# Output and down products with the tokens stationary in a linear-attention kernel gated by a Hadamard feed-forward net

## The chip, the cores and the metric

The kernel runs on one core of one Trainium2 chip. All numbers are 32-bit floats. The metric is device time in microseconds, the median of some runs; beside it stands one execution under the hardware profiler, whose span is the time from the first to the last instruction.

The engines are TensorE (PE, matrix products into PSUM; its weight loads are counted apart as PEld), VectorE (DVE), ScalarE (ACT), GpSimd (POOL) and SyncE (SP), which issues nearly all of this kernel's transfers.

## The reference

`x` has the shape (8, 512, 512): 8 batches of 512 tokens of 512 features. After a layer norm there are two branches, and the result is a gated residual. `fwht` is the normalized Walsh-Hadamard transform over the features.

```python
xn = layernorm(x)
# branch s: linear attention
q, k, v = xn @ Wq.T + bq, xn @ Wk.T + bk, xn @ Wv.T + bv
kv = cumsum((elu(k) + 1) * v, axis=tokens)              # elementwise
s = ((elu(q) + 1) * kv * 32 ** -0.5) @ Wo.T + bo
# branch g: feed-forward net, 512 -> 2 x 2048 -> 512
h = fwht(xn * SU_ug)
h = silu((h @ W_gate.T) * Wscale_gate) * ((h @ W_up.T) * Wscale_up)
h = fwht(h * SU_dp)
g = silu((h @ W_down.T) * Wscale_dp)
out = x + s * g
```

## The kernel before

**Tiling.** The batches are worked off in four pairs `p`; the two batches of a pair are the two sides `s` of a 2x2 block product. Each product is done as a Strassen-Winograd scheme: seven products P1 to P7 of blocks stand for eight, and sums before and after are done on other engines. The contraction is cut in units of 2 x 128 features, of which attention and the output projection have two and down has eight (four in each half).

**A group.** `group` (L265) makes one pair of 128-wide output tiles for all tokens: for each of the seven products a 128x128 block of the weight is loaded as the stationary side and 512 tokens move past it (the matmul is L277). Results have features on the partitions and tokens in the columns. The PSUM tile `px` (three banks) gathers P1, P6, P5 and P3 one after another, and its state is read in between as `sa`, `sb`, `sc` (on ScalarE at L289 or, with a bias added, at L291; on VectorE at L287 where an earlier half is added). `py` (one bank) takes P2, `pz` (two banks) takes P7 and P4; VectorE adds them to the snapshots (L295). A further pair of PSUM banks is tagged `t`, for transposes and for the folding of weights.

**Order.** An agenda (`at`, `advance`) places the seven products of a group in time, so that products of neighbouring groups lie between each other and snapshots are ready when they are needed; its unit is the product of one 128x128 block with 512 tokens. Within that, a scheduler that knows dependencies and priorities fixes the order on each engine; `background()` marks work of a lower priority. Each engine then follows its own list in order and waits at each instruction for what it needs.

**Weights.** `get_w` takes the next weight from a list in the order of use and asks for three ahead (`ask`). In the first pair weights come raw from the input, are encoded for the seven products (`encode_weights`, L175 to L179), and the encoded form is stored to HBM; later pairs read it back (`later_w`). For gate and up the Hadamard transform is folded into the weights: butterflies on VectorE, one product with the 128x128 Hadamard matrix `had` on TensorE (`pw`), a copy with scale on ScalarE. For down the same is done on four blocks `o` of 128 output columns: `butterflies_down` (its load of `rd` from HBM L691, its butterflies L646 and L647) and `fold_down` (the product `pwd` L702, the copies L708, the store to `wd_f` L711). `between`, called after each group, counts groups: at 0, 3, 6 and 9 it puts butterflies, at 2, 5, 8 and 11 a fold. In later pairs gate and up use a two-level scheme with 256 moving columns (`block_product`, product L364), and their weights are streamed.

**Output projection and down.** `project_out` makes two groups `g` with the bias from ScalarE, and stores `o` to HBM. In the first pair it stands after the first gate group. `down` makes two groups in each of two halves of the hidden features. The first half's sum is stored to HBM; it is fetched again with `s` and `x` (as `y`) before the second half. The first group of each half has an `early` part, contraction units that can be multiplied before the last hidden unit `ho` is there (3 of 4 in the first pair, else 2). In the second half each quarter of `d` gets the Silu with the scale `wsc_c` (ScalarE, L604) and is multiplied with `s` (L607, on POOL for g = 0 and VectorE for g = 1). `finish` (L632) then turns the product to rows of tokens with 32 transposes `po` (L638), adds `y` on VectorE (L639) and stores 8 times 256 KB.

**Transfers.** All loads and stores but a few constants are issued on SP's queue, in one order; an issue that waits for data holds up those behind it. The pool `t8` has six buffers of 1 MB each, `wpool` four for weights; x of the next pair has one buffer.

## Time and profile before

| | |
|---|---|
| median of 3 runs | 1608.95 us (1608.57 to 1610.97) |
| profiled execution | 1611.34 us, span 1609.6 us |
| mean granted clock of TensorE | 0.992 |
| TensorE busy | 1559.2 us in 4944 instructions |
| VectorE busy | 920.8 us in 1314 |
| ScalarE / POOL busy | 452.4 / 475.6 us |
| moved by DMA | 246.30 MB, q1 45.3% of 16 engines |
| stores of out | 32 of 256 KB |

A group's row gives the line, the engine and the operation, the output and the inputs by the program's names, the shape and the count, then busy time, the mean of one in ns, the engine's idle time just before and what ended it. A row of the chain gives start, duration and what ran or landed. A matmul of 32-bit floats stands in the trace as two instructions. The mean duration of a matmul includes its latency; what counts is the distance between starts.

### The profile page before, as it was taken

Reading aid. Unit: us, or ns where it says so; the run is one execution under the profiler, and the core shown is the slowest. Engines: PE = TensorE matmul, PEld = TensorE weight load, DVE = VectorE, ACT = ScalarE, POOL = GpSimd, SP = SyncE. Lnnn points to the kernel's source line nnn. Section 1 sums busy time; section 2 is a strip of 40 time slices with the busy share of each in tenths; the row PEclk is TensorE's granted clock in tenths of the full one; section 3 lists DMA queues with packets and bytes.
Section 4 is the critical chain, followed back from the end, with each engine's and each line's share of the span. In section 5 each row is a group of like instructions: output and inputs, shape, how many; then the busy total and the mean of one; then the engine's idle time right before and its main releaser. Section 6 shows DMA issues by size and latency. Waiting matters only on the chain.

```text
span 1609.6 us, 13688 instructions
## 1 busy us (share of the span) xinstructions
PE 1559.2 (97%) x4944; PEld 918.3 (57%) x4944; DVE 920.8 (57%) x1314; ACT 452.4 (28%) x712; POOL 475.6 (30%) x272
## 2 busy tenths in 40 slices
PE   5988999999999999999999999999999999999998
PEld 2433444444444486758844476847854466856864
DVE  5886665266576573716675473625675475543673
ACT  2543431133133432111223432111221442111211
POOL 4442044004410243304610235301620226110630
PEclk9999999999999999999999999999999999999999
DMA  8333855255853244426554134525564133515471
GB/s 249 119 91 98 257 166 171 96 184 159 277 206 142 71 140 162 140 72 209 191 202 166 69 119 136 186 82 176 186 226 144 69 114 115 190 69 193 157 271 53
DMA packets 142675, 246.30 MB, mean 153 GB/s; under 512 B 7952, under 2 KB 107280, under 8 KB 138512
## 3 DMA queue, kind: packets, MB, share of 16 engines
q1 hardware_dynamic: 141408, 245.39, 45.3%
q8 instruction: 39, 0.64, 0.2%
q10 hardware_dynamic: 1200, 0.04, 0.0%
q14 instruction: 28, 0.23, 0.0%
HBM read 175.67 MB, written 69.73 MB: 152 GB/s over the span
## 4 chain that ended last, share of the span: by engine, by line
PE 90%; DMA 3%; DVE 3%; POOL 1%; issue 1%; ACT 1%; SPq 0%; ACTq 0%; DVEq 0%; POOLq 0%
PE px_gu L364 18%; PE px_dn L277 12%; PE pz_gu L364 9%; PE pz_dn L277 7%; PE py_gu L364 5%; PE px_o L277 3%; PE px_up L277 3%; PE px_k L277 3%; PE px_gate L277 3%; PE px_v L277 3%; PE px_q L277 3%; PE py_dn L277 3%; PE pz_o L277 2%; PE pz_up L277 2%; PE pz_gate L277 2%; PE pz_k L277 1%
## 5 line engine op out<-in xcount | busy, mean ns | idle before, releaser
L277 PE MATMUL px_dn<-ho,w_down 128*128 128x512 f32 x512 | 234.5, 601 | 0.6 <-DVE sc_dn L287 0.6
L277 PEld LDWEIGHTS px_dn<-ho,w_down 128*128 128x128 f32 x512 | 97.9, 193 | 116.1 <-issue 110.1
L564 POOL TENSOR_TENSOR u<-u,v 128x1024 f32<-128x1024 f32 x24 | 56.1, 2363 | 352.8 <-DVE u L402 198.0
L277 PE MATMUL pz_dn<-ho,w_down 128*128 128x512 f32 x256 | 117.4, 599 | 4.8 <-POOL ho L172 4.8
L452 POOL TENSOR_TENSOR v<-v,k 128x1024 f32<-128x1024 f32 x16 | 40.8, 2552 | 190.2 <-ACT v L427 161.9
L277 PEld LDWEIGHTS pz_dn<-ho,w_down 128*128 128x128 f32 x256 | 48.0, 191 | 60.8 <-issue 50.9
L277 PE MATMUL px_o<-co,w_o 128*128 128x512 f32 x128 | 60.2, 601 | 7.5 <-DVE co L462 7.5
L277 PE MATMUL px_v<-xo,w_v 128*128 128x512 f32 x128 | 62.0, 608 | 4.9 <-ACT sc_v L291 4.9
L526 POOL TENSOR_TENSOR ho<-g,u 128x512 f32<-128x512 f32 x8 | 11.3, 1410 | 182.8 <-DVE u L295 182.8
L277 PE MATMUL px_k<-xo,w_k 128*128 128x512 f32 x128 | 63.0, 608 | 1.0 <-ACT sc_k L291 1.0
L568 POOL TENSOR_TENSOR v<-v,r 128x1024 f32<-128x1024 f32 x24 | 56.2, 2361 | 25.6 <-DVE r L402 25.6
L607 POOL TENSOR_TENSOR s<-s,d 128x512 f32<-128x512 f32 x16 | 22.4, 1403 | 139.3 <-ACT d L604 139.3
L604 ACT ACTIVATE d<-d,wsc_c 128x512 f32<-128x512 f32 x32 | 23.1, 722 | 140.0 <-DVE d L295 118.6
L277 PE MATMUL px_q<-xo,w_q 128*128 128x512 f32 x128 | 60.1, 592 | 0.0
L277 PE MATMUL px_gate<-xo,w_gate 128*128 128x512 f32 x128 | 60.0, 592 | 0.0
L277 PE MATMUL px_up<-xo,w_up 128*128 128x512 f32 x128 | 59.2, 592 | 0.0
L277 PE MATMUL py_dn<-ho,w_down 128*128 128x512 f32 x128 | 58.5, 592 | 0.0
L554 ACT ACTIVATE a<-a,cols_sb 128x512 f32<-128x512 f32 x24 | 17.3, 722 | 144.1 <-DVE a L402 142.5
L454 DVE TENSOR_TENSOR_SCAN k<-ones,v 128x512 f32<-128x512 f32 x32 | 38.4, 1240 | 33.5 <-POOL v L452 33.5
L549 POOL TENSOR_TENSOR ho<-ho 128x1024 f32<-128x1024 f32 x24 | 56.4, 2359 | 1.4
L554 ACT ACTIVATE v<-v,cols_sb 128x512 f32<-128x512 f32 x24 | 17.3, 722 | 102.8 <-POOL v L568 102.8
L554 ACT ACTIVATE u<-u,cols_sb 128x512 f32<-128x512 f32 x48 | 34.2, 722 | 42.3 <-DVE u L402 39.8
(742 smaller groups left out, 3264.0 us busy)
## 6 DMA issues: line engine op xcount, KB each, us to landing
w_down<-d_down SPq DMA_DIRECT2D x24, 896.0 KB, 4.6
d_s<-o SPq DMA_DIRECT2D x8, 1024.0 KB, 7.4
d_d<-dn SPq DMA_DIRECT2D x8, 1024.0 KB, 9.3
d<-d_d SPq DMA_DIRECT2D x8, 1024.0 KB, 6.2
s<-d_s SPq DMA_DIRECT2D x8, 1024.0 KB, 8.7
y<-in_x_dram SPq DMA_DIRECT2D x8, 1024.0 KB, 8.2
out_dram<-y SPq DMA_DIRECT2D x32, 256.0 KB, 5.4
d_gu<-s_gate SPq DMA_DIRECT2D x16, 448.0 KB, 4.5
```

What stands on the lines that cost most here:

```text
L277: nc.tensor.matmul(p.rearrange("p a t -> p (a t)") if len(r.shape) == 2 else p, ws[k][:, i, :], r, start=(first and k == 0), stop=(k == n ...
L364: nc.tensor.matmul(p[:, lane], w[:, lane, i, :], x[:, i, :], start=(first and lane == 0), stop=True, skip_group_check=True,)
L452: nc.gpsimd.tensor_tensor(v[:, h], v[:, h], k[:, h], ALU.mult)
L454: nc.vector.tensor_tensor_scan(k[:, h, s], ones.to_broadcast([P, L]), v[:, h, s], 0.0, ALU.mult, ALU.add)
L526: nc.gpsimd.tensor_tensor(ho[:, P1], g[:, 0, 0], r[:, 0, 0], ALU.mult)
L549: eng.tensor_tensor(ho[:, :, c], ho[:, :, a], ho[:, :, b], ALU.subtract)
L554: nc.scalar.activation(g[:, m], g[:, m], AF.Silu, scale=col("w_gate", u + m * NU + a * NG))
L564: nc.gpsimd.tensor_tensor(r[:, m], ru1[:, m], rv[:, m], ALU.add)
L568: nc.gpsimd.tensor_tensor(rv[:, m], rv[:, m], rr[:, m], ALU.add)
L604: nc.scalar.activation(d[:, o, s], d[:, o, s], AF.Silu, scale=wsc_c[:, g + 2 * o : g + 2 * o + 1])
L607: eng.tensor_tensor(r[:, o, s], r[:, o, s], d[:, o, s], ALU.mult)
```

## The change

Both `project_out` and `down` no longer use `group` but a new function, `token_groups`. Now 128 tokens of the attention output (or of `ho`) are the stationary side and 256 columns of the weight move past them, so that results come in rows of tokens. Two groups `g` of 256 tokens each (`c` is the half of them) go side by side with their own px, py and pz. `finish` goes: in down's second half the Silu is followed by the product with `s` and the addition of `y` on the same layout, and each 256 tokens are stored with one transfer of 512 KB. Since features now lie along the columns, `bo` is held as a row, broadcast to all partitions, and added by VectorE when px is read (L402 of the new file; L400 is the ScalarE copy without bias); Wscale_dp is multiplied into down's weight by VectorE ahead of the butterflies (L795), from a row broadcast of 128x128 (L791), and the constant 2048^-0.5 moves into `su_dp`. The load of `rd` leaves `butterflies_down` and becomes `load_down`, called two groups earlier; a `plan` by group count says when loads, butterflies and folds come. Down's weights are brought to the form by factor by `down_w` in the first pair, stored, and streamed in all four pairs as 512 KB a factor (56 loads; before 24 of 896 KB in the later pairs, and 8 weights raw in the first). In the first pair the output projection stands after the second gate group instead of the first.

```diff
-    bo_c = const.tile([P, KD], F32, tag="bo_c", name="bo_c")
-    wsc_c = const.tile([P, KD], F32, tag="wsc_c", name="wsc_c")
+    bo_r = const.tile([P, D], F32, tag="bo_r", name="bo_r")
+    wsc_r = const.tile([P, P], F32, tag="wsc_r", name="wsc_r")
...
+    def rows_w(w, src, n0, dn):
+        for a in range(2):
+            for b in range(2):
+                n = n0 + b * dn
+                nc.sync.dma_start(
+                    w[:, (P1, P2, P7, P4)[2 * a + b]], src[n * P : (n + 1) * P, a * 2 * P : (a + 1) * 2 * P]
+                )
+    wd = [dram.tile([P, 7, 4, 2 * P], F32, tag=f"d_down_{h}", name=f"d_down_{h}") for h in range(2)]
+    def down_w(u, j):
+        t = t8.tile([P, 2, 7, P], F32, tag="t", name=f"wd_{u}_{j}")
+        w = by_factor(t)
+        rows_w(w, wd_f, u + NU * j, NG)
+        def encode():
+            encode_weights(nc.vector, w)
+            nc.sync.dma_start(wd[u // 2][:, :, 2 * (u % 2) + j], w)
+        at(8, encode)
...
+    def token_groups(name, n, tok, wts, dst, add=None, early=None, done=None):
+        px, py, pz = {}, {}, {}
+        sums, ws = {}, {}
+        def product(p, i, g, first, ks=None):
+            if i not in ws:
+                ws[i] = wts(i)
+            for k in ks or range(n):
+                t = tok(k, i)
+                for c in range(2):
+                    nc.tensor.matmul(
+                        p[:, c], t[:, (2 * g + c) * P : (2 * g + c + 1) * P], ws[i](k),
+                        start=(first and k == 0 and c == 0), stop=(k == n - 1), skip_group_check=True,
+                    )
+        def read(what, o, a, s, g):
+            if o is None:
+                o = snap.tile([P, 2, 2 * P], F32, tag="s", name=f"{what}_{name}_{g}")
+            if add is None:
+                nc.scalar.copy(o, px[g])
+            else:
+                nc.vector.tensor_tensor(o, px[g], add(a, s, g), ALU.add)
+            return o
+        def output(o, p, a, s, g):
+            nc.vector.tensor_tensor(dst(a, s, g), o, p, ALU.add)
+            if done:
+                done(a, s, g)
...
+        steps = [(p, g) for p in (p1, p7) for g in range(2)]
+        place = 0
+        if early:
+            a, b = range(early), range(early, n)
+            for p, g in steps:
+                at(place, lambda p=p, g=g: p(g, a))
+                place += early
+            place = max([place] + [e[0] - now[0] for e in agenda])
+            for p, g in steps:
+                at(place, lambda p=p, g=g: p(g, b))
+                place += n - early
+            steps = []
+        steps += [(p2, 0), (p6, 0), (p2, 1), (p6, 1)]
+        steps += [(p, g) for p in (p5, p3, p4) for g in range(2)]
...
+        def gated(a, s, g):
+            d, r, y = (block(t[s], a, g) for t in (ds, ss, ys))
+            nc.scalar.activation(d, d, AF.Silu)
+            last = p == B // 2 - 1 and (a, s) == (1, 0)
+            (nc.vector if last else nc.gpsimd).tensor_tensor(r, r, d, ALU.mult)
+            nc.vector.tensor_tensor(y, y, r, ALU.add)
+            parts[s, g] = parts.get((s, g), 0) + 1
+            if parts[s, g] == 2:
+                nc.sync.dma_start(
+                    out[2 * p + s, 2 * g * P : (2 * g + 2) * P].rearrange("(n p) d -> p n d", p=P),
+                    ys[s][:, 2 * g : 2 * g + 2],
+                )
...
-    def finish(p, ss, ys):
-        for s in (1, 0):
-            for t in range(NT):
-                y = ys[s][:, t]
-                pt = ps.tile([P, KD, P], F32, tag="t", name=f"po_{p}_{s}_{t}")
-                for o in range(KD):
-                    nc.tensor.transpose(pt[:, o, :], ss[o % 2][:, o // 2, s, t * P : (t + 1) * P], ident)
-                nc.vector.tensor_tensor(y, y, pt.rearrange("p o t -> p (o t)"), ALU.add)
-                nc.sync.dma_start(out[2 * p + s, t * P : (t + 1) * P, :], y)
...
+    def load_down(o, rs):
+        r = rs[:, o % 2]
+        nc.sync.dma_start(r, wdown_t[:, o * P : (o + 1) * P].rearrange("(c p) e -> p c e", p=P))
+        nc.sync.dma_start(wsc_r, wscale_dp[o * P : (o + 1) * P].partition_broadcast(P))
     def butterflies_down(o, rs):
         r, r2 = rs[:, o % 2], rs[:, 2]
-        nc.sync.dma_start(r, wdown_t[:, o * P : (o + 1) * P].rearrange("(c p) e -> p c e", p=P))
+        nc.vector.tensor_tensor(r, r, wsc_r.unsqueeze(1).to_broadcast([P, NF, P]), ALU.mult)
...
+    plan = {}
+    for o, (n, a, b) in enumerate(((0, 0, 2), (2, 4, 6), (4, 6, 8), (6, 8, 10))):
+        plan.setdefault(n, []).append(lambda o=o: load_down(o, rs))
+        plan.setdefault(a, []).append(lambda o=o: rd.update({o: butterflies_down(o, rs)}))
+        plan.setdefault(b, []).insert(0, lambda o=o: fold_down(o, rd[o]))
+    for n, u, j in ((10, 0, 0), (10, 0, 1), (11, 1, 0), (11, 1, 1), (16, 2, 0), (17, 2, 1), (18, 3, 0), (19, 3, 1)):
+        plan.setdefault(n, []).append(lambda u=u, j=j: down_w(u, j))
     def between():
-        n = groups[0]
+        for step in plan.pop(groups[0], []):
+            with background():
+                step()
         groups[0] += 1
-        if n % 3 == 2 and n // 3 < 4:
-            fold_down(n // 3, rd[n // 3])
-        if n % 3 == 0 and n // 3 < 4:
-            with background():
-                rd[n // 3] = butterflies_down(n // 3, rs)
...
                 gs = [gate(p, u, xo, get_w)]
+                gs.append(gate(p, u + NU, xo, get_w))
                 if u == 0:
                     project_out(p, co, get_w)
-                gs.append(gate(p, u + NU, xo, get_w))
```

## The prediction

> **What bounds the kernel now.** I read the page's busy times and clock first, then the chain that ended last, then the chain in single stretches, then the groups and the waits. Busy times and the chain's shares:
>
> ```profile
> PE 1559.2 (97%) x4944; PEld 918.3 (57%) x4944; DVE 920.8 (57%) x1314; ACT 452.4 (28%) x712; POOL 475.6 (30%) x272
> PE 90%; DMA 3%; DVE 3%; POOL 1%; issue 1%; ACT 1%; SPq 0%; ACTq 0%; DVEq 0%; POOLq 0%
> ```
>
> TensorE is the bound. Only two things move the time: the length of its instruction sequence, and its idle gaps. The pace, start to start, comes from long unbroken pieces of the chain (start, us, what): late products of down, of gate and up, and the transposes of a next pair's x.
>
> ```profile
> 1564.37 6.87 PE px_dn L277 x16
> 1327.84 1.73 PE px_gu L364 x8
> 832.61 0.88 PE pt L142 x8
> ```
>
> So 512 columns cost 6.87/16 = 0.429 us, 256 columns 1.73/8 = 0.216, a 128x128 transpose 0.11. All 4944 instructions at such paces make about 1539 of the span's 1609.6 us. The other 71 are 16 before the first instruction, a tail of some 10, about 6 of first transposes, and stalls of the first pair (some 30) and at the two later pair changes (7). The largest stall, from the chain between 120 and 145 us:
>
> ```profile
> 122.75 6.63 DMA wd_f<-rd
> ...
> 129.44 5.44 DMA rd<-in_wdown_t_dram
> ...
> 134.91 0.04 DVE rd L646
> ...
> 136.05 1.22 DVE q L440
> 137.27 1.15 DVE co L462
> ...
> 138.45 2.07 PE px_o L277 x2
> ```
>
> The load of the next 128 columns of down's weight stands on SP's queue behind the store of the ones before; VectorE waits with a butterfly, the attention output behind it, and TensorE stands 7.65 us (130.80 to 138.45). VectorE's two such waits:
>
> ```profile
> L646 DVE TENSOR_TENSOR rd<-rd 128x1024 f32<-128x1024 f32 x16 | 21.3, 1330 | 13.2 <-DMA rd<-in_wdown_t_dram 13.0
> ```
>
> **Part 1, the transposes of the output go** (L638, L639).
>
> ```profile
> L638 PE MATMUL po<-ident,s 128*128 128x128 f32 x128 | 18.8, 277 | 1.4 <-DVE y L639 1.4
> L639 DVE TENSOR_TENSOR y<-y,po 128x512 f32<-128x512 f32 x32 | 20.7, 681 | 1.3 <-PE po L638 1.0
> ```
>
> Three pairs have 96 of them in the sequence: 96 x 0.11 = **-10.5 us** (at a mean occupancy of 0.139 I find for po, -13). The adds remain, of the same size (L713). For the last pair the tail counts:
>
> ```profile
> 1596.32 3.45 PE pz_dn L277 x8
> ...
> 1605.05 1.29 DVE y L639 x2
> ```
>
> The last product ends at 1599.77, the span 9.8 later. After: output add 0.69, Silu 0.72 (L604's mean), multiply 0.69 (VectorE's L607), add 0.69, and a store of 512 KB, which I put at 4 from the 3.3 that the last 256 KB take (1606.34 to 1609.6): 7.0, hence **-2.8**. A gap of 0.73 us at 1592.6 and two transposes placed early go as well: **-0.9**.
>
> **Part 2, 256 moving columns for 512** in output and down products: (896 + 224) x 0.4293 = 480.8 becomes 2240 x 0.2157 to 0.2163 = 483.2 to 484.4: **+3.0**. Here the row must be weighed against the Trainium skill. "TensorE: Matmul & The Clock Gate", section "Back-to-back issue gap", says that in a stream of weight load and matmul both set the spacing: 81 ns for 128 columns where the matmul alone would take 56. A load exposed by 25 ns on each of 2240 would be +56 us and a kernel slower by 3%. The row L364 above is such a stream, one 128x128 load for each 256 columns, and shows 0.216, just half of 0.429; loads take 0.19 and fit under it. I take the row. That tokens are now the stationary side changes no shape.
>
> **Part 3, first pair, attention.** Each load of `rd` but the first is asked for two groups before its use (`load_down`). The two waits of 13.0 us go, and with them the gap of 7.65 and some 1.4 of slow clock behind it. Against that, VectorE gets a multiply of 128x2048 for each of four blocks (scale into the weights): two 128x1024 operations of 1.22 each (L646's usual time) are 2.4 us, two blocks lie in attention: 4.9. VectorE is full there already (10.0 of 10 us busy in 90 to 100 and in 100 to 110), and the gate's butterflies, two groups earlier now, add 2 to 3. SP carries a broadcast of 64 KB more for each block. A part of the idle time comes back as VectorE work: I take **-8**, ends -15 and 0.
>
> **Part 4, folds closer together.** In the built order several products with the Hadamard matrix (`pwd`, `pw`) stand together on TensorE. They share two `t` banks, emptied by ScalarE in four pieces at 0.27 to 0.38 us, 1.1 to 1.5 a bank, against 0.43 of product. Four such runs lose at most 1 + 1.2 + 1.2 + 2.4 = 5.8; they lose nothing where ScalarE is ahead. I take **+3**.
>
> **Part 5, output projection of the first pair.** Its px reads with the bias move from ScalarE (0.69) to VectorE (0.69), behind butterflies of 1.2 to 1.5 us; 3 px banks hide one such delay, not two in a row. 0 to +4.5; I take **+2**. In later pairs products of the hidden unit lie between (the chain at 1371 to 1391 us alternates px_o with px_gu): nothing.
>
> **Part 6, down in the first pair.** The weights are encoded in rows, stored and streamed back by factor; the chain is the same, wd_f store, load of its rows, encode. VectorE waits in it already:
>
> ```profile
> DVE w_down L176 <- DMA w_down<-wd_f: 24.3, 7, 5.5
> ```
>
> It costs little today; TensorE's own stalls around both halves come from POOL:
>
> ```profile
> PE pz_dn L277 <- POOL ho L172: 4.8, 2, 2.5
> ```
>
> Half 0: from -1.5 (more early products before ho is needed) to +5 (an encode that waits for its load holds the outputs queued behind it on VectorE): **0**. Half 1: in the new order the 32 transposes of x_2 stand some 20 us earlier on TensorE, ahead of the last product of px_up, so the layer norm must be done earlier. Today it ends just in time:
>
> ```profile
> 456.69 0.56 DVE x L129
> ...
> 457.29 1.11 PE pt L142 x8
> ```
>
> Behind them wait the last products of up, and then ho on POOL. A new stall of 3.5 to 7.5, less the 2.6 at 441 which is absorbed: **+3**, ends 0 and +8.
>
> A second rule matters for all these stalls. The same page, "HAM oscillation", allows gaps up to about 3.4 us before the clock halves; then stalls of 1 to 2.5 us cost just themselves. This trace, by windows (stretch, its length, busy times and counts, clock):
>
> ```profile
> 278.00:284.00 6.00, 5.59 (x9) 2.46 (x10) 2.55 (x4) 0.59 (x1) 1.75 (x2) 0.72 0.37 153
> ```
>
> A gap of 2.47 us ended at 278.40; then 9 instructions ran where 13 fit: 1.7 us lost more. (One of 2.89 us at 1201 left the clock at 1.00.) Parts 3 to 6 by the rule alone would be some 2 us lower; the values taken include one slow clock.
>
> **Part 7, later pairs.** Down's weights come in 512 KB a factor, needed each 16 x 2 x 0.216 = 6.9 us; 448 KB take 4.5 us to land, and three are asked ahead: hidden. If that cover were gone, 7 x 4.5 a half is as much as the products take, so a late load would show at once. At pair changes the transposes of the second next x stand 1.6 us of work earlier; they wait 2.04 and 2.89 us today for a load of 7.7 to 8.6: **+2.5** for both. Of the 32 multiplies s*d POOL gets 30 at 1.40 where it had 16; 8 in the some 48 us of a half's products leave it idle time, and VectorE is spared 14 at 0.69: nothing on the path, except that the last pair's final part stays on VectorE (in the tail above).
>
> **Sum.** -10.5 - 2.8 - 0.9 + 3.0 - 8 + 3 + 2 + 0 + 3 + 2.5 = -8.7. The span becomes 1600.9, and the profiled run's 1611.34 about 1602.6. The runs' median is 2.4 below that run, so 1608.95 - 8.7 = **1600 us**. The certain part (transposes, tail, columns) is -11.2; the first pair is a wash with wide ends.
>
> **Rivals.**
> - *A cleaner first pair* (0.24): prefetch takes all of parts 3's stalls (-14) and parts 4 to 6 cost only 3. -11.2 - 14 + 3 + 2.5 = -20: about 1589. For it: VectorE idles 13.0 us on loads alone. Against: it is full in the stretch between.
> - *A cancelled gain* (0.20): parts 4 to 6 come out high, +13 together with -5 for part 3: -11.2 + 8 + 2.5 = -1, about 1608. For it: all three need VectorE in the first 200 us, where it has least room.
> - *Slower* (0.14): the wait for wd_f. Today's 24.3 us are borne because the early part of down and three px banks cover them. In the new plan encodes of 8 tiles come up in the middle of gate and up, whose gates and outputs use VectorE too; each wait of up to 5.5 us then stops all products once banks are full. Four uncovered (22 us) less 8 of cover from banks is +14, which gives -8.7 + 14 = +5, 1614; it decides from about 12 us of uncovered wait on.
> - The likeliest (0.42) has 1594 to 1606 as its own range.
>
> A measurement can tell about 0.2%, 3.2 us, from no change. Faster by more: 0.42 + 0.24 + 0.08 of the cancelled gain = 0.74; within: 0.12; slower: 0.14. Range 1586 to 1613: from the good end of part 3 to the middle of the slower case.
>
> **What would show it.** No po group; 2240 of 256 columns at 0.216 for px, py, pz of o and dn (if 0.24 or more, part 2 fails and the kernel is slower). VectorE's wait for rd near 0 and the gap at 138 us gone; if TensorE still waits for VectorE's co there, part 3 was busy time, not waiting. TensorE waits for ScalarE's rd (part 4), for VectorE's sa_o and sb_o (5), for ho or pt<-x around 440 us (6). The last product to the end in 7 us. Wrong above all if the waits for the w_down rows grow beyond 24 us and show up as TensorE gaps.

## The result, and where the time went

The changed kernel takes 1605.55 us (median of 10 runs, 1602.12 to 1606.69); beside it the kernel before took 1609.41 (10 runs, 1607.73 to 1612.96). The ratio is 0.9971, with a 95% interval of 0.9961 to 0.9980: faster by 0.29%, 4.7 us. The forecast was 1600 us, 8.95 less. The sign is right and the size is half, and the parts behind it are not those of the forecast. The profiled execution took 1606.13 us, its span 1604.3 (before 1611.34 and 1609.6).

**The page after.** Busy time, share of the span and instructions of each engine:

```profile
PE 1550.9 (97%) x5936; PEld 1117.1 (70%) x5936; DVE 949.2 (59%) x1335; ACT 425.1 (26%) x679; POOL 504.9 (31%) x286
```

And the shares of the chain that ended last:

```profile
PE 73%; DVE 12%; DMA 5%; issue 4%; POOL 3%; ACT 2%; SPq 1%; POOLq 0%; DVEq 0%; ACTq 0%
```

TensorE has 992 instructions more and is busy 8 us less. VectorE is busy 28 us more, and its share of the chain went from 3% to 12%: more of the chain that sets the end runs over VectorE now.

**The two parts that came as forecast.** The chain of the changed kernel in down of the third pair, in a hidden unit behind it, and at the end (start, us, what):

```profile
1071.34 17.27 PE px_dn L391 x80
1102.50 1.73 PE px_gu L475 x8
...
1597.76 0.61 DVE d L406
...
1599.78 0.69 DVE y L713
```

Eighty instructions of 256 columns (two to a product), each with a weight load of its own, take 17.27 us: 0.2159 each, the forecast's row and not the higher price that the rule of the Trainium skill ("TensorE: Matmul & The Clock Gate", section "Back-to-back issue gap") would have given. The loads last 0.19 us and still fit. From the output add of the last product (1597.76) to the end of the span (1604.3) it is 6.5 us, about 7 from the product's own end.

**A ledger by stages.** To see where the rest went, I take for an instruction of TensorE its start less the sum of the paces (0.4293, 0.216, 0.109 us for 512, 256 and 128 columns) of all instructions ahead of it: its lateness. The growth of the lateness over a stage is what TensorE lost there to waiting and to a slow clock. (A gap is given below as the growth of the lateness over it, which is 0.1 to 0.2 us more than the idle time in the waits.) From the two profiled executions, in us:

| stage | before | after | change | forecast |
|---|---|---|---|---|
| instructions at their paces | 1538.8 | 1527.9 | -10.9 | -11.0 |
| start, up to the first product of k | 19.8 | 15.6 | -4.3 | 0 |
| attention, first gates, output projection | 24.2 | 23.6 | -0.5 | -6 (parts 3 and 5) |
| up and gate groups with the folds, up to down | 0.0 | 15.0 | +15.0 | +3 (part 4) |
| down, first half, and the groups behind it | 4.7 | 1.7 | -3.0 | 0 |
| down, second half, and change to pair 2 | 5.2 | 6.6 | +1.4 | +3 |
| the two other changes of pair | 8.8 | 6.6 | -2.3 | +2.5 |
| last pair and tail | 8.2 | 7.7 | -0.5 | -0.2 |
| span | 1609.6 | 1604.3 | -5.2 | -8.7 |

(The transposes of the last pair, 3.5 us, stand in the first row here; the forecast had them in its tail. Rounding makes 0.1.) Three rows decide: a gain at the start of which the forecast says nothing, attention with -0.5 instead of -6, and 15 us in a stage that had lost nothing. Each column is one execution. In run 3 below, which changes only when loads of the first pair are asked for, the rows with the change to pair 2 and with the two other changes read 3.5 and 6.2 where the kernel before has 5.2 and 8.8; so differences of 2 to 3 us in these two rows show nothing.

**The start.** The chain from the first transfer to the first products, of before and then of after:

```profile
1.67 7.80 DMA wsc_c<-in_wscale_dp_dram
...
9.49 0.17 DVE wsc_c L804
9.66 1.19 DVE st L122 x2
```

```profile
1.23 6.85 DMA x<-in_x_dram
...
8.10 1.29 DVE st L122 x2
...
11.67 3.75 PE pt L142 x16
```

Before, one small multiplication of the scale column (L804) stood on VectorE ahead of the layer norm and waited for a load of single 4-byte elements. The change drops that instruction, since the scale goes into the weights, and the layer norm starts with the arrival of x.

**The 15 us.** TensorE's waits in the changed kernel (us in total, times, longest):

```profile
...
PE pz_q L316 <- DVE q L332: 7.9, 2, 4.3
PE px_up L316 <- DVE w_up L178: 4.0, 1, 4.0
PE pz_gate L316 <- DVE g L332: 3.6, 1, 3.6
PE px_v L316 <- ACT sc_v L328: 3.5, 1, 3.5
PE px_k L316 <- ACT sa_k L328: 3.4, 3, 2.3
...
PE pwd L806 <- ACT rd L812: 2.0, 3, 1.3
```

The forecast's mechanism for this stage, folds that wait for ScalarE, is the last line (with 1.0 us more for `pw_gate` and `pw_up`; 2.0 of these 3.0 us lie in this stage). The large ones of this stage, px_up at 203 us and pz_gate at 228 us, wait for VectorE. By the ledger the first costs 5.9 us with the slow clock behind it, the second 5.5, and the pieces with the folds 3.6. The chain ahead of the first, and VectorE's list in that stretch (start, us, line, operation, what):

```profile
174.06 5.16 DMA wd_f<-rd
...
179.30 7.53 DMA rd<-in_wdown_t_dram
...
186.85 0.03 DVE rd L795
...
202.48 0.34 DVE w_up L178
```

```profile
186.85 2.29 DVE L795 TENSOR_TENSOR rd<-rd,wsc_r 128x2048 f32<-128x2048 f32 x1 [1.66 <-DMA rd<-in_wdown_t_dram]
...
190.25 1.98 DVE L745 TENSOR_TENSOR rd<-rd 128x1024 f32<-128x1024 f32 x1
192.16 3.37 DVE L746 TENSOR_TENSOR rd<-rd 128x1024 f32<-128x1024 f32 x1
...
199.86 1.48 DVE L177 TENSOR_TENSOR w_up<-w_up 128x256 f32<-128x256 f32 x1
...
202.40 0.41 DVE L178 TENSOR_TENSOR w_up<-w_up 128x256 f32<-128x256 f32 x1
```

The load of block 3 of down's weight is issued at 179.30 us, behind the store of block 1; before it was issued at 129.44. Its butterflies, which began at 134.91 in the kernel before, ahead of the attention output, now stand among the up groups, ahead of the encoding (L177, L178) of a weight that TensorE needs next.

VectorE's list ahead of the second gap is another one. The butterflies of block 3 end at 211 us. What stands ahead of the gate's output `g` are butterflies of a weight of up (L759 to L762), which begin late, behind a load:

```profile
222.08 1.66 DVE L759 TENSOR_TENSOR r_up<-w_up 128x512 f32<-128x512 f32 x1 [2.72 <-DMA w_up<-in_wup_t_dram]
223.66 1.75 DVE L760 TENSOR_TENSOR r_up<-w_up 128x512 f32<-128x512 f32 x1
225.45 1.64 DVE L761 TENSOR_TENSOR r_up<-r_up 128x512 f32<-128x512 f32 x1
...
227.61 0.68 DVE L332 TENSOR_TENSOR g<-sc_gate,pz_gate 128x512 f32<-128x512 f32 x1
```

Block 1's store is 51 us later than before (122.75). Block 0's is 45 us later, though its places in the plan are the old ones. SP's list, before and after:

```profile
69.68 0.37 SPq L711 DMA_DIRECT2D wd_f<-rd  x1
...
114.32 0.38 SPq L815 DMA_DIRECT2D wd_f<-rd  x1
```

The diff shows a change that the plan's numbers do not: the folds were outside `background()` and are inside it now. Block 0's first fold product starts at 98.5 us where it started at 57.9, and at 95.7 in the run without the multiplications (number 4), so these are not the reason. No run puts the folds back to their old priority, so what it costs is not known.

### The profile page after: what moved, and what is told of

Same layout as the page of the kernel before. It is cut to its first block, busy times and chain, and to the rows that moved or that the text cites. A ratio compares the mean times of both kernels' runs of the same rounds, so it can differ in the third digit from the quotient of the medians.

```text
span 1604.3 us, 15681 instructions
## 1 busy us (share of the span) xinstructions
PE 1550.9 (97%) x5936; PEld 1117.1 (70%) x5936; DVE 949.2 (59%) x1335; ACT 425.1 (26%) x679; POOL 504.9 (31%) x286
## 4 chain that ended last, share of the span: by engine, by line
PE 73%; DVE 12%; DMA 5%; issue 4%; POOL 3%; ACT 2%; SPq 1%; POOLq 0%; DVEq 0%; ACTq 0%
PE px_gu L475 18%; PE pz_gu L475 9%; PE px_dn L391 8%; PE py_gu L475 5%; PE pz_dn L391 4%; PE px_o L391 3%; PE px_v L316 3%; PE px_k L316 3%; PE px_q L316 3%; PE py_dn L391 2%; DMA x<-in_x_dram 2%; POOL s L712 2%; PE pz_o L391 2%; PE pz_q L316 2%; PE pz_k L316 1%
## 5 line engine op out<-in xcount | busy, mean ns | idle before, releaser
L475 PE MATMUL px_gu<-xo,w_gu 128*128 128x256 f32 x1344 | 320.6, 380 | 0.0
L475 PEld LDWEIGHTS px_gu<-xo,w_gu 128*128 128x128 f32 x1344 | 254.7, 190 | 39.9 <-issue 3.6
L391 PE MATMUL px_dn<-w_down,ho 128*128 128x256 f32 x1024 | 230.1, 379 | 2.2 <-DVE sb_dn L402 1.7
L391 PEld LDWEIGHTS px_dn<-w_down,ho 128*128 128x128 f32 x1024 | 193.6, 190 | 31.4 <-DVE sb_dn L402 2.7
L475 PE MATMUL pz_gu<-xo,w_gu 128*128 128x256 f32 x672 | 173.1, 380 | 0.0
L475 PEld LDWEIGHTS pz_gu<-xo,w_gu 128*128 128x128 f32 x672 | 127.0, 190 | 19.1 <-DVE a L517 0.9
L391 PE MATMUL pz_dn<-w_down,ho 128*128 128x256 f32 x512 | 116.6, 380 | 1.9 <-POOL ho L172 1.9
L391 PEld LDWEIGHTS pz_dn<-w_down,ho 128*128 128x128 f32 x512 | 96.4, 190 | 17.6 <-POOL ho L172 2.7
L475 PE MATMUL py_gu<-xo,w_gu 128*128 128x256 f32 x336 | 86.2, 379 | 0.0
L475 PEld LDWEIGHTS py_gu<-xo,w_gu 128*128 128x128 f32 x336 | 63.9, 190 | 8.7
```

Of the source, the lines that this page charges most:

```text
L391: nc.tensor.matmul(p[:, c], t[:, (2 * g + c) * P : (2 * g + c + 1) * P], ws[i](k), start=(first and k == 0 and c == 0), stop=(k == n - 1), ...
L475: nc.tensor.matmul(p[:, lane], w[:, lane, i, :], x[:, i, :], start=(first and lane == 0), stop=True, skip_group_check=True,)
```

## Experiments

Each kernel was timed in five rounds beside the kernel before. Ratios are to that kernel (1608.4 to 1610.0 us in the four sets); 0.9971 is the changed kernel's. Two theories stand against each other. The first: VectorE in the first pair has no room, so the amount of work that the change gives it (the multiplications L795) is what TensorE loses. The second: it is the places in the plan, and what a load waits for, that put VectorE's work where TensorE needs it.

**1. The start alone.** The kernel before, without L804:

```diff
-    nc.vector.tensor_tensor(su_dp, col("su_dp", 0, NF), col("w_up", 0, NF), ALU.mult)
-    nc.vector.tensor_scalar(wsc_c, wsc_c, FF ** -0.5, None, ALU.mult)
+    nc.vector.scalar_tensor_tensor(
+        su_dp, col("su_dp", 0, NF), FF ** -0.5, col("w_up", 0, NF), ALU.mult, ALU.mult
+    )
```

> The kernel before, with one VectorE instruction less: the multiplication of wsc_c by 2048^-0.5 at L804 is dropped and the constant goes into su_dp, as in the changed kernel. In the trace of before the layer norm stands behind L804 on VectorE, which waits until 9.49 us for a load of single 4-byte elements (7.80 us); in the trace of after the layer norm starts at 8.10 us and TensorE 4.16 us earlier. Theory (that one wait is the whole gain of the start): first TensorE instruction at about 11.7 us, time 4.2 us less than before, about 1605. Rival (x arrives earlier because the scattered small loads are gone, or it differs from run to run): no gain here.

Measured: 1603.42 us, ratio 0.9954 (0.9942 to 0.9966). The first TensorE instruction comes at 10.60 us (before 15.83), the first product of k is 6.6 us less late. The small scattered loads are still issued here; only the waiting instruction is gone, so the rival falls. This one line in the old kernel is worth at least as much as the whole change. Since the changed kernel has this gain in it too, everything else in it adds up to about nothing.

**2. The transposes alone.** The kernel before, with y added to the product as it lies:

```diff
-                pt = ps.tile([P, KD, P], F32, tag="t", name=f"po_{p}_{s}_{t}")
-                for o in range(KD):
-                    nc.tensor.transpose(pt[:, o, :], ss[o % 2][:, o // 2, s, t * P : (t + 1) * P], ident)
-                nc.vector.tensor_tensor(y, y, pt.rearrange("p o t -> p (o t)"), ALU.add)
+                nc.vector.tensor_tensor(y, y, ss[t % 2][:, t // 2, s], ALU.add)
```

> The kernel before with the transposes of the output left out: finish adds the untransposed product to y, so the output is not the reference's. This prices part 1 alone. Theory of the prediction: 96 x 0.11 = 10.5 us less in three pairs and about 3.5 to 4 less at the end, where add and store follow the last product at once: 13 to 15 us less than before, about 1595. Rival (the transposes covered a wait at each change of pair, which now opens, as the changed kernel's waits for sa_k at 498, 869 and 1238 us suggest): 4 to 7 of it come back, 6 to 10 us less than before.

Measured: 1599.39 us, ratio 0.9936 (0.9922 to 0.9949): 10.2 us less than the 1609.61 beside it. The instructions are 14.0 us shorter. Some comes back at a change of pair, as the rival said, though not in its wait (none for sa_k shows): the transpose of the next x at 827 us now waits 3.69 us where it waited 2.04, and this change costs 8.1 us of lateness instead of 4.8. The chain of that wait begins with the load of x (7.74 us before, 8.96 here), which does not get shorter when the work ahead of it does. With the scatter of these rows, the amount is not firm.

**3. The prefetch alone.** The kernel before, with `load_down` called after groups 1, 4 and 7 and no multiplication:

```diff
     def butterflies_down(o, rs):
         r, r2 = rs[:, o % 2], rs[:, 2]
-        nc.sync.dma_start(r, wdown_t[:, o * P : (o + 1) * P].rearrange("(c p) e -> p c e", p=P))
...
+        if n == 0 or n in (1, 4, 7):
+            with background():
+                load_down((n + 2) // 3, rs)
```

> The kernel before with part 3's first half alone: each load of rd but the first is asked for two groups before its butterflies. No multiplication is added. Theory (VectorE's waits of 13.0 us for rd were waits, so that without them the gap of 7.65 us before px_o goes with its slow clock): 7 to 10 us less than before, about 1601; VectorE's wait for rd near 0. Rival (VectorE has a backlog at that place and the loads were only the last to end): 1 to 4 us less, the gap before px_o still there, released by co.

Measured: 1609.65 us, ratio 1.0000 (0.9992 to 1.0009). No gain at all, and the gap before px_o is there (6.02 us). Its chain:

```profile
122.71 6.60 DMA wd_f<-rd
...
129.37 5.42 DMA rd<-in_wdown_t_dram
...
138.36 2.08 PE px_o L277 x2
```

The load is issued at 129.37 us instead of 129.44. The theory falls. The gap stays and is released by co, as the rival had it, but for another reason: the load was not asked for too late, it had no place to go. `rs` has two slots for blocks, and block 3 must wait for the store of block 1 whenever it is asked for.

**4. The multiplications left out, or done elsewhere.** The changed kernel without L795 (down's weights then lack their scale):

```diff
-        nc.vector.tensor_tensor(r, r, wsc_r.unsqueeze(1).to_broadcast([P, NF, P]), ALU.mult)
```

> The changed kernel without the four VectorE multiplications L795, so that down's scale is left out of the output. They take 2.2 to 3.3 us each, 9 to 10 in all. Theory (VectorE is full in the first 230 us and each us of work there is a us of TensorE's stalls): 8 to 14 us less than the changed kernel, the gaps at 203 and 228 us gone or halved. Rival (the gaps come from waits for loads and for POOL's use of memory, not from the amount of VectorE's work): at most 4 us less, both gaps there.

Measured: 1595.15 us, ratio 0.9909 (0.9896 to 0.9922), 10 us less than the changed kernel. The four instructions are busy 10.2 us: by the medians VectorE's time is TensorE's time here, as the first theory has it. But the two gaps did not go:

```profile
PE pz_gate L316 <- DVE g L332: 3.5, 1, 3.5
PE px_up L316 <- DVE w_up L178: 3.5, 1, 3.5
```

Of the 9 us of lateness that went, 5.7 went up to the first up group, in attention and the projection, where three of the four stand with 7.9 us, and hardly any in the stage of the 15 us (14.6 instead of 15.0); another 2.1 went at the change to pair 2, within its scatter. So the cost of the multiplications and the 15 us are two things. Two attempts to do the same scaling elsewhere. The first, on POOL, stands on the plan of number 5 (1595.23):

```diff
-        nc.vector.tensor_tensor(r, r, wsc_r.unsqueeze(1).to_broadcast([P, NF, P]), ALU.mult)
+        nc.gpsimd.tensor_tensor(r, r, wsc_r.unsqueeze(1).to_broadcast([P, NF, P]), ALU.mult)
```

> The earlier plan of loads, butterflies and folds, with the multiplication by Wscale_dp on POOL instead of VectorE. A POOL operation of 128x1024 takes 2.36 us, so 4.7 for 128x2048. Theory of amount (VectorE's 9 to 10 us are the cost): 5 to 10 us less than with it on VectorE (1595), about 1587. Rival (POOL slows VectorE's operations that read only SBUF, 1.22 to 1.73 us on average for 128x1024, and butterflies then wait longer for the product): within 3 us of 1595.

Measured: 1606.58 us, ratio 0.9983 (0.9973 to 0.9994): 11 us worse. TensorE's gap at 70 us before pz_q, 3.6 us on VectorE, becomes 10.62, and the one at 144 us 8.36. The four multiplications last 4.5 to 5.6 us on POOL, and butterflies of VectorE beside them up to 4.94, so the rival's reason is there, and costs more than it said.

The second scales the product instead of the weights, before the Silu, in the changed kernel; the scale's row is loaded into bo's tile once the first pair's projection is done, and bo again for each next pair:

```diff
-        nc.vector.tensor_tensor(r, r, wsc_r.unsqueeze(1).to_broadcast([P, NF, P]), ALU.mult)
...
-            nc.scalar.activation(d, d, AF.Silu)
-            last = p == B // 2 - 1 and (a, s) == (1, 0)
-            (nc.vector if last else nc.gpsimd).tensor_tensor(r, r, d, ALU.mult)
+            last = p == B // 2 - 1 and (a, s) == (1, 0)
+            eng = nc.vector if last else nc.gpsimd
+            eng.tensor_tensor(
+                d, d, bo_r[:, a * 2 * P : (a + 1) * 2 * P].unsqueeze(1).to_broadcast([P, 2, 2 * P]), ALU.mult
+            )
+            nc.scalar.activation(d, d, AF.Silu)
+            eng.tensor_tensor(r, r, d, ALU.mult)
...
+            nc.sync.dma_start(bo_r, bo.partition_broadcast(P))
...
+        nc.sync.dma_start(bo_r, wscale_dp.partition_broadcast(P))
```

> The changed kernel with Wscale_dp taken out of down's weights (no L795): the sum of down is multiplied by a broadcast row of it on POOL before the Silu (VectorE for the last part of the last pair), 32 more operations of about 1.4 us where POOL is idle; the row shares a tile with bo and is loaded again for each pair. Theory (the multiplications on VectorE in the first pair cost what a_nomul showed, 10.4 us, and POOL has room in down's second half): 6 to 10 us less than the changed kernel, about 1597. Rival (the longer way Silu has to wait opens the gap at the change of pairs, where ScalarE's sa_k stands behind Silu): 3 changes of pair at 1.4 to 2.8 us each and 0.7 at the end, 1 to 5 us less.

Measured: 1633.96 us, ratio 1.0153 (1.0139 to 1.0166): 28 us worse than the changed kernel, worse than the rival said. In the first 425 us it gained 9 us of lateness (the kernel without the multiplications 6); it lost all that and more at the changes of pair and in the tail. Its row for the wait that costs 3.4 us in the changed kernel:

```profile
PE px_k L315 <- ACT sa_k L327: 26.0, 3, 9.5
```

ScalarE's copy of the next pair's first product stands behind the last Silus of the pair before, and each Silu now waits for POOL, as ScalarE's list at the first change shows:

```profile
495.13 0.63 ACT L714 ACTIVATE d<-d 128x512 f32<-128x512 f32 x1 [4.28 <-POOL d L711]
495.67 0.67 ACT L327 ACTIVATE sa_k<-px_k,cols_sb 128x512 f32<-128x512 f32 x1
```

It shows large what the changed kernel has small: at each change of pair the gating chain stands ahead of k. With the plan of number 5 added the same kernel took 1628.73 (ratio 1.0120, 1.0105 to 1.0136):

> Both last edits together: scale after down's sum, and folds at the places of the kernel before. Theory (both act on VectorE's crowding, in different places): 10 to 16 us less than the changed kernel, about 1592. Rival (each removes the same backlog): no more than the better of the two alone.

The sum of both was not reached: the plan's gain on top of it is 5 us here.

**5. The places in the plan.** The changed kernel, with only these places changed:

```diff
-    for o, (n, a, b) in enumerate(((0, 0, 2), (2, 4, 6), (4, 6, 8), (6, 8, 10))):
+    for o, (n, a, b) in enumerate(((0, 0, 2), (2, 3, 5), (4, 6, 8), (7, 9, 11))):
...
-    for n, u, j in ((10, 0, 0), (10, 0, 1), (11, 1, 0), (11, 1, 1), (16, 2, 0), (17, 2, 1), (18, 3, 0), (19, 3, 1)):
+    for n, u, j in ((11, 0, 0), (11, 0, 1), (12, 1, 0), (12, 1, 1), (16, 2, 0), (17, 2, 1), (18, 3, 0), (19, 3, 1)):
...
-        at(8, encode)
+        encode() if u == 1 else at(8, encode)
```

> The changed kernel with butterflies and folds at the places of the kernel before, or one group beside (loads, butterflies, folds after groups 0,0,2; 2,3,5; 4,6,8; 7,9,11), and the rows of down's weight one group later. All else as changed. Theory (the place of the last two blocks' butterflies, in the middle of the up groups, makes the stalls of 6.0 and 7.6 us around 203 and 228 us): those two fall by half or more, 4 to 10 us less than the changed kernel. Rival (the amount of work on VectorE, wherever it stands): stalls appear elsewhere before 270 us, within 3 us of the changed kernel.

Measured: 1595.23 us, ratio 0.9914 (0.9901 to 0.9928): 9 to 10 us less than the changed kernel, with the same work. The stage of the 15 us now costs 6.9. The two halves of the edit, each alone (the second moves block 3 and, with it, the rows of down's weight and their encoding):

> The changed kernel with one place moved: butterflies and fold of block 1 after groups 3 and 5 (as in the kernel before) instead of 4 and 6; the rest of the plan as changed. Theory from the traces: rd has two buffers for loaded blocks, so the load of block 3 waits for the store of block 1 whenever it is asked for. Before, it was issued at 129 us, in the changed kernel at 179 us, and block 3's butterflies fell into the up groups. Then this edit alone brings the load back to about 140 us, the stalls of 6.0 and 7.6 us around 203 and 228 us fall by half or more, 5 to 10 us less than the changed kernel, about 1597. Rival (the place of block 3 itself decides): within 3 us of the changed kernel.

> The changed kernel with the other half of the earlier edit alone: block 3's load, butterflies and fold after groups 7, 9 and 11 instead of 6, 8 and 10 (and the rows of down's weight one group later); block 1 stays at 4 and 6. Theory (block 1's store holds block 3's load): load still near 179 us, within 3 us of the changed kernel, or slower. Rival (block 3's place decides): 5 to 10 us less.

Measured: block 1 alone 1598.77, ratio 0.9928 (0.9916 to 0.9940); the other half 1601.86, ratio 0.9947 (0.9935 to 0.9958). The stage costs 8.8 and 13.2 us. SP's list with block 1 moved (start, us, line, what):

```profile
135.63 0.38 SPq L815 DMA_DIRECT2D wd_f<-rd  x1
140.19 0.38 SPq L790 DMA_DIRECT2D rd<-in_wdown_t_dram  x1
```

and the wait of TensorE that it left over of the two:

```profile
PE pz_gate L316 <- DVE g L332: 3.5, 1, 3.5
```

The same two views with block 3 moved, first SP's list:

```profile
173.76 0.37 SPq L815 DMA_DIRECT2D wd_f<-rd  x1
178.89 0.37 SPq L790 DMA_DIRECT2D rd<-in_wdown_t_dram  x1
```

then the wait left over:

```profile
PE px_up L316 <- DVE w_up L178: 3.8, 1, 3.8
```

With block 1 back at groups 3 and 5, its store leaves at 135.63 instead of 174.06 us, the load of block 3 follows at 140.19, and the gap at 203 us is gone. With the other half, the load stays at 178.89 and that gap stays, but the one at 228 us goes. So the theory held for the first gap only. The second is not one of block 3's butterflies: with block 1 moved these end at 174 us, and the gap, now at 223 us, stands behind the same butterflies of up's weight (216.31 to 222 us). What in the other half removes it, block 3's fold or the rows of down's weight, stays open. The gains, 6.8 and 3.7 us by the medians, add up to the 10.3 of both. Both expectations were too simple: each of the two edits removes one gap.

**6. POOL beside VectorE.** In the trace of the changed kernel VectorE's operations of 128x1024 with both inputs in SBUF last 1.218 us on average where POOL does nothing (48 of them), and 1.732, at most 3.368, where POOL works for over 80% of the time (16); those of 128x512 with an input from PSUM last 0.686 and 0.687 (436 and 259). The Trainium skill says the same in "SBUF — State Buffer", section "Who interferes with whom": a VectorE instruction with two SBUF inputs contends with a GpSimd instruction that reads SBUF, one with a single SBUF input does not. To see what it costs, the encoding on POOL was put off:

```diff
-            encode_tokens(nc.gpsimd, ho)
+            if f % NU:
+                encode_tokens(nc.gpsimd, ho)
+            else:
+                at(100, lambda: encode_tokens(nc.gpsimd, ho))
```

> The changed kernel with POOL's four encoding subtractions of the first hidden unit (two sets) put off by 100 units (43 us), away from VectorE's butterflies at 186 to 212 us. In the trace of after these butterflies last 1.98 to 3.37 us beside POOL's work where 1.22 is usual without it. Theory (POOL and VectorE slow each other when both read SBUF): butterflies near 1.3 us, gap at 203 us down from 4.2 to 2 or less, 3 to 7 us less than the changed kernel. Rival (VectorE simply has too much to do, or waits for the fold's ScalarE copies): gaps unchanged, within 2 us of the changed kernel.

(In this kernel the early products P7 of the first hidden unit take rows that are not encoded yet.) Measured: 1601.41 us, ratio 0.9951 (0.9934 to 0.9968), 3 to 4 us less than the changed kernel, with intervals that overlap; the gap at 203 us is 2.07 instead of 4.18. But the edit did not do what it was made for: the scheduler left three of the first set's four subtractions where they were, and the butterflies beside them are as long as before (3.36 us the longest). Only the encoding of w_up behind them went from 1.48 to 0.41 us. That POOL lengthens VectorE's work is shown by the durations; what it costs the kernel in all is not. POOL is a rival for part of the gap at 203 us: the first four butterflies of block 3 last 9.8 us there (1.98, 3.37, 2.17, 2.28), where four take 4.9 without POOL, and the run with block 1 moved takes them away from POOL (1.21 to 1.23 each) as well as from the up groups.

**7. The projection back ahead of the second gate.** On the plan of number 5, and with bo loaded on SP after group 1:

```diff
-                at_o = len(queue) - (2 if p == 0 else 0)
+                at_o = len(queue) - (3 if p == 0 else 0)
...
-                gs.append(gate(p, u + NU, xo, get_w))
                 if u == 0:
                     project_out(p, co, get_w)
+                gs.append(gate(p, u + NU, xo, get_w))
```

> The earlier plan, with the output projection of the first pair back after the first gate group (as in the kernel before) and the broadcast of bo loaded on SP after the first group instead of beside x. Prices the move of the projection, costed at nothing by the prediction. Theory (the second gate group covers the wait for co): 4 to 8 us more than 1595, with a gap before px_o of 5 us or more as before. Rival (VectorE's backlog is the same in either order): within 2 us of 1595. The first TensorE instruction about 1 us earlier than 11.6 in both cases.

Measured: 1604.45 us, ratio 0.9966 (0.9953 to 0.9979): 9 us more than 1595.23, although it starts 1.6 us earlier (first TensorE instruction at 10.03 us), and 9.6 more than 1594.85, the same plan with bo's load moved alike (number 8). The move of the projection, costed at nothing, is worth about 10 us on this plan: in the old order its products wait for VectorE's output of the same projection, 9.46 us at 172 us. The wait for co is small there (2.42 us, on POOL), so the expectation named the wrong wait, and its 4 to 8 us were a little low.

**8. The multiplications behind attention.** They move to the row tiles of `down_w`, in two operations for each tile, ahead of its encoding, with the scale's row in bo's tile after group 9; beside it the base, which is the plan of number 5 with only the load of bo moved:

```diff
-        nc.vector.tensor_tensor(r, r, wsc_r.unsqueeze(1).to_broadcast([P, NF, P]), ALU.mult)
...
         def encode():
+            for a, f in enumerate((slice(P1, P2 + 1), slice(P7, P4 + 1, P4 - P7))):
+                row = bo_r[:, a * 2 * P : (a + 1) * 2 * P].unsqueeze(1).to_broadcast([P, 2, 2 * P])
+                nc.vector.tensor_tensor(w[:, f], w[:, f], row, ALU.mult)
             encode_weights(nc.vector, w)
...
+    plan.setdefault(9, []).append(lambda: nc.sync.dma_start(bo_r, wscale_dp.partition_broadcast(P)))
...
+            nc.sync.dma_start(bo_r, bo.partition_broadcast(P))
```

The base's edit:

```diff
-    nc.scalar.dma_start(bo_r, bo.partition_broadcast(P))
...
+    plan.setdefault(1, []).append(lambda: nc.sync.dma_start(bo_r, bo.partition_broadcast(P)))
```

> The earlier plan (1595) with the multiplication by Wscale_dp moved to down_w: two VectorE operations of 128x1024 on each of the eight row tiles just before their encoding, from a row that shares a tile with bo; bo is loaded after the first group. The multiplied elements are as many as before (16 x 1.2 us = 20 us if at 128x512 rate, about the same 9 to 10 us of elements), but behind the attention. Theory of place (VectorE has no slack in attention and some behind the first up groups): 5 to 9 us less than the earlier plan, about 1588. Theory of amount (each us of VectorE's work before 430 us is a us of TensorE's stall): same as the earlier plan, or 5 to 10 more where the operations cost 20 us.

> The earlier plan with the broadcast of bo loaded on SP after the first group instead of on ScalarE's queue beside x. All theories: first TensorE instruction at 10.0 us instead of 11.6, 1.5 us less than the earlier plan, about 1594; it serves as the base of the run beside it.

Measured: 1591.35, ratio 0.9891 (0.9874 to 0.9908), against 1594.85, ratio 0.9904 (0.9887 to 0.9921) for the base. (The operations were built as 16 of 128x512, not of 128x1024, and are busy 12.6 us.) The intervals overlap, so place alone is not shown to help. In the trace 4 us of lateness are saved up to the first up group, and 1.5 of them come back at 266 us, where down's products wait 2.15 us for a weight that is encoded and stored later; the two profiled spans are 1593.2 and 1592.8. Of the base, the first TensorE instruction at 9.74 us shows the 1.9 us that bo's load beside x costs; the time can't tell it from number 5.

The plan of number 5 with either of these beats both kernels: 1591 to 1595 us, 14 to 17 less than before.

## Why the forecast was wrong

**Part 3 failed, -8 forecast with the projection's +2 beside it, -0.5 measured for the two.** Its signs came true: VectorE's waits for `rd` fell from 13.0 to 1.7 us (and 2.2 for `wsc_r`), and the gap before px_o went. But "the two waits of 13.0 us go" was put down to the earlier load, and run 3 shows that asking earlier alone changes nothing (1.0000), because the load waits for a slot. And the time came back in the same stage. The forecast's own figures were 9.05 less for the gap and its clock (the ledger has 1.8 for the clock, not 1.4), 4.9 more for the multiplications and 2 to 3 for the gate's butterflies, which leaves -1.6; the -8 holds only if nearly all the added work falls into idle time. Run 4 prices the multiplications at 10 us for 10.2 us of instructions, 5.7 of it here. In the place of the old gaps stand those before pz_q at 63 and 107 us (3.7 and 4.5, the old one 1.1) and before pz_o at 151 (3.2), all behind VectorE. What the stage did gain goes with the moved projection (run 7), which I had costed at nothing.

**Part 4 failed in its mechanism, +3 forecast, +15 measured.** I looked for waits on ScalarE between folds that stand together, and those are 3.0 us, as forecast. The two large gaps wait for VectorE, of which that part says nothing. Behind the first is a moved block of butterflies that I never placed in time: block 1's store left 51 us later, the load of block 3 with it (179 for 129 us), and VectorE's work fell where it delays TensorE (POOL beside it may have a part, number 6). Putting block 1's fold back by one group returns 38 of these 51 us and takes the gap away (run 5). The second gap goes with the other half of that edit, for a reason that stays open. With both, 6.9 of the 15.0 us are left.

**What was not in the sum.** The start gave -4.3. The forecast spoke of the 16 us before the first instruction and went on; the chain from 0 to 16 us has L804 in it, and the diff deletes L804. That the sign came out right is luck: without this gain the sum would be near nothing.

**Right.** Part 1's transposes and the tail by count (10.2 us alone in run 2, part of it given back to a transfer), part 2's pace (0.2159), and that the skill's higher price for narrow products doesn't hold here. The rival of a wait for wd_f did not come: VectorE waited 1.6 us for those rows in the changed kernel, where it was 24.3 before. The streamed weights of down stayed hidden too (TensorE waits for none of them), though the forecast's check of it was off: 7 x 4.5 us are 31.5 a half, not the 48 that the products take.

**Parts 6 and 7** forecast +3 and +2.5; the ledger has -1.6 and -2.3, of which the scatter of the changes of pair may be the most. In part 6 the stall of 2.61 us at 441 fell to 0.74, and x_2's transposes waited 0.89, not 3.5 to 7.5. In part 7 the second next x did not come late, and a smaller wait took its place, px_k for ScalarE's sa_k behind the Silus.

**The clock.** At that wait of the changed kernel (stretch, length, busy times and counts, clock):

```profile
496.00:502.00 6.00, 4.23 (x6) 1.89 (x7) 2.46 (x4) 1.76 (x3) 2.64 (x2) 0.72 0.81 300
```

A gap of 2.44 us was followed by half the clock, and cost 4.1 us in all; at the gaps of 203 and 228 us it was 1.8 more each. The Trainium skill ("TensorE: Matmul & The Clock Gate", section "HAM oscillation") has the clock lowered by gaps above some 3.4 us. By that rule 2.44 would have cost only itself. A gap above it, 3.69 us before px_v at 90 us, left the clock full:

```profile
89.80:92.00 2.20, 2.16 (x5) 1.06 (x6) 2.20 (x3) 0.64 (x2) 0.00 (x0) 1.00 0.00 0
```

So did one of 1.10 us at 869. Between 2.4 and 3.7 us the length of a gap did not tell here what the clock does.

## What to carry to other kernels

Place moved work in time, not only in amount: for each load that is asked for earlier, find what frees its buffer, and follow that store; a prefetch without a free slot is no prefetch. When a diff deletes an instruction, look in the chain for what stood behind it, at the start of the kernel above all. And where an engine off the bound is full in one stretch, count work added there at nearly its whole time: idle time that a wait made goes with that wait. And read a diff for changes of priority too, not only of place.

## What the runs showed of the hardware

VectorE's operations with both inputs in SBUF ran 1.4 times as long beside POOL (1.218 and 1.732 us for 128x1024, at most 3.368), those with an input in PSUM not at all longer (0.686 and 0.687). Gaps of TensorE of 2.44 us (at 496) and 3.69 us (at 90) were followed by half the clock and by the full one. In the kernel before, a load of 512 single elements of 4 bytes took 7.80 us; in the changed one, x's 512 KB took 6.85.
